# Attention in larger batches: regrouping the score and value steps of one layer, and sharing the softmax totals of four heads

## The chip, the cores and the metric

The kernel runs on one core of a Trainium2 chip. The metric is the device time of one execution in microseconds (us). The whole network is in float32, and every matrix product below is a float32 product.

The engines are named as the profile names them: PE is TensorE (its matrix products), PEld is TensorE loading the stationary operand, DVE is VectorE, ACT is ScalarE, POOL is GpSimd. PSUM is the memory that TensorE writes its products into; here it has eight banks, each 128 partitions by 512 float32 numbers.

## The reference, cut to what matters

The network has four layers for 8 samples of 512 channels by 32 x 32 positions. Only layer 0 is changed. Its attention has 8 heads of 64 channels over 1024 positions:

```python
h = group_norm(x, gn_scale, gn_bias)
qkv = jnp.einsum('oc,bchw->bohw', qkv_w, h) + qkv_b[None, :, None, None]
q, k, v = (to_heads(t) for t in jnp.split(qkv, 3, axis=1))      # 8 heads of 64
attn = jax.nn.softmax(jnp.einsum('bnsd,bntd->bnst', q, k) * hd ** -0.5, axis=-1)
h = jnp.einsum('bnst,bntd->bnsd', attn, v)
h_flat = h.transpose(0, 1, 3, 2).reshape(B, C, S).transpose(0, 2, 1)
for _ in range(3):                                               # lax.scan
    h_flat = h_flat + 0.1 * jnp.tanh(jnp.einsum('bsc,oc->bso', h_flat, inl_w) + inl_b)
h = h_flat.transpose(0, 2, 1).reshape(B, C, H, W)
x = x + jnp.einsum('oc,bchw->bohw', proj_w, h) + proj_b[None, :, None, None]
```

Layers 1 to 3 (another attention, an up- and downsampling filter, a convolution with mixed experts) follow and are as before.

## The kernel before

The exponentials are taken without subtracting a maximum. So the kernel looks at the sums it divides by: whatever is larger than a bound, or not a number, makes a second program run that subtracts the maximum. It collects what is to be looked at in `seen`. With these inputs the second program does not run.

For each sample, the attention of layer 0 is cut into 8 **groups**. A group is two heads (one on partitions 0 to 63, the other on 64 to 127) and one half (512) of the query positions. A group has 8 **steps**, one for each 128 key positions. A step computes the transposed scores (keys on partitions, queries along the free axis), their exponentials `e`, adds `e` to the group's running sum `acc` and multiplies `e` with the values. A "scores" product has 64 rows of the array for each head, so the two heads share the array by rows; an "av" product has 64 columns for each head, so they share it by columns.

```python
ps_sc = ...tile_pool(bufs=2, PSUM)   # 2 pairs of banks: [128, 1024]
ps_tp = ...tile_pool(bufs=2, PSUM)   # 2 single banks:   [128, 512]
ps_mm = ...tile_pool(bufs=2, PSUM)   # 2 single banks:   [128, 512]
def tmp(name, n=HALF):               # e: 5 buffers of [128, 1024]
    ...
def sums(name):                      # acc: 2 buffers of [128, 1024]
    return work.tile([P, S], F32, tag="sums", name=name, bufs=2)

# ---- in layer0 ----
groups = [(oc, sh) for sh in range(2) for oc in range(CC)]

def scores(t):
    g, jc = divmod(t, SC)                                   # SC = 8
    oc, sh = groups[g]
    ps = ps_sc.tile([P, S], F32, tag="scores", ...)         # a pair of banks
    scores_T([ps[:, ts(r, HALF)] for r in range(2)], ...)   # 64 x 128 by 64 x 512, both heads
    e = tmp(f"e_{b}_{t}", S)
    nc.scalar.activation(e, ps, AF.Exp, scale=HD ** -0.5)
    exps[t] = e
    if jc == 1:
        accs[g] = sums(f"acc_{b}_{g}")
        nc.vector.tensor_add(accs[g], exps[t - 1], e)
    elif jc > 1:
        nc.vector.tensor_add(accs[g], accs[g], e)

def weighted(t):
    ...
    for r in range(2):                                      # 128 x 64 by 128 x 512, both heads
        nc.tensor.matmul(avs[g][rows[r]], v[:, jc, ts(2 * oc + r, HD)], e[:, ts(r, HALF)],
                         start=(jc == 0), stop=(jc == SC - 1))

def normalised(g):
    oc, sh = groups[g]
    acc = accs.pop(g)
    ps = bank(ps_tp, f"total_{b}_{g}")
    for r in range(2):                                      # sums over the partitions
        nc.tensor.matmul(ps[rows[r]], ones[:, 0:HD], acc[:, ts(r, HALF)], start=True, stop=True)
    inv = tmp(f"inv_{b}_{g}", HALF)
    nc.vector.reciprocal(inv, ps)
    nc.vector.tensor_mul(hf[:, oc, ts(sh, HALF)], avs.pop(g), inv)
    for part in (acc[:, 0:HALF], acc[:, HALF:S], inv):
        nc.gpsimd.tensor_add(seen, seen, part)

n = len(groups) * SC
for t in range(0, n + 4, 2):            # two steps of scores, then the two steps of av before them
    for u in (t, t + 1):
        if u < n: scores(u)
    for u in (t - 2, t - 1):
        if 0 <= u < n: weighted(u)
    if t >= SC + 2 and (t - 2) % SC == 0:
        normalised((t - 2) // SC - 1)
```

After the attention come three "inl" products and "proj". Each multiplies 512 x 512 weights with the 512 x 1024 `hf` in seven products of quarters, not eight (Strassen's scheme in Winograd's form). The data side needs four sums of quarters, each in two parts, written by `quarter_sums`; for the first of the three, they are written over `v`:

```python
for cc in range(2):                      # in quarter_sums
    b11, b12 = src[:, cc, 0:HALF], src[:, cc, HALF:S]
    b21, b22 = src[:, cc + 2, 0:HALF], src[:, cc + 2, HALF:S]
    nc.vector.tensor_sub(t[0][cc], b12, b11)
    nc.vector.tensor_sub(t[1][cc], b22, t[0][cc])
    nc.vector.tensor_sub(t[2][cc], b22, b12)
    nc.vector.tensor_sub(t[3][cc], t[1][cc], b21)

order = (                                # in product: result, banks, weights, data (a number: that sum)
    ("P1", "A", "A11", b11), ("C11", "A", "A12", b21), ("U2", "X", "S2", 1),
    ("U3", "X", "S3", 2), ("C22", "Y", "S1", 0), ("C21", "X", "-A22", 3),
    ("C12", "Y", "S4", b22),
)
```

The framework in which the kernel is written places semaphores and buffers, and also chooses the order of instructions on each engine: it is near the order of the text, but an instruction whose buffer or input is not there yet by the framework's own estimate can be put behind a later one.

## Time and profile before

| | |
|---|---|
| time, median of 3 runs | 3939.58 us (3938.11 to 3940.49) |
| span of the profiled run | 3934.4 us |
| PE busy | 3868.2 us (98%) |
| DVE busy | 2593.8 us (66%) |
| ACT busy | 1105.0 us (28%) |
| POOL busy | 436.1 us (11%) |
| granted TensorE clock, mean | 0.998 |

The busy time of PE is a union: where two products share the array, their common time counts once. A busy PE is not an array that is full. The chain of waits follows the program back from its last instruction, at each step to what released it; the shares say on which engine's work the end rests. Rows of groups give the source line, the engine, the operation, the tiles written and read, the shapes, the count, the total busy time and the mean duration of one, and then the idle time of the engine just before them. In a timeline each row is a run of like instructions: start, length, engine, what it is, and in brackets the idle time before it and what ended that.

### The profile page before, as it was taken

The numbers are of one execution on the slowest core, as the hardware profiler recorded it, in microseconds if no ns is written. First come the engines' busy times: TensorE is split into PE (matmuls) and PEld (weight loads), VectorE is DVE, ScalarE is ACT, GpSimd is POOL, SyncE is SP. The second block draws the span as 40 slices with busy tenths as digits, with TensorE's granted clock in tenths as the row PEclk, the third lists the DMA queues.
The fourth block names the chain that finished last, engine by engine and source line by source line (L and its number), as shares of the span: only waits on it lengthen the run. The fifth ranks groups of instructions, "written<-read, shape, count | busy, mean of one in ns | idle before, by whom it ended". The sixth has DMA issues, their size and how long they took to land.

```text
span 3934.4 us, 37957 instructions
## 1 busy us (share of the span) xinstructions
PE 3868.2 (98%) x14630; PEld 2032.6 (52%) x14630; DVE 2593.8 (66%) x3690; ACT 1105.0 (28%) x1507; POOL 436.1 (11%) x310
## 2 busy tenths in 40 slices
PE   8999999999999999999999999999999999999998
PEld 4336653476435763366434754357534764346543
DVE  4777848764686647775586646765487655766786
ACT  1421224212332114212241123322142122421333
POOL 5310003000120003100030002200031001301000
PEclk9999999999999999999999999999999999999999
DMA  5002310122101310023101221013200131003432
GB/s 197 19 0 83 115 57 1 40 77 100 38 0 59 118 68 11 0 83 115 56 1 59 79 81 37 1 70 107 78 1 24 60 115 57 1 0 112 164 134 103
DMA packets 85792, 247.86 MB, mean 63 GB/s; under 512 B 10480, under 2 KB 33024, under 8 KB 78816
## 3 DMA queue, kind: packets, MB, share of 16 engines
q1 hardware_dynamic: 69712, 220.23, 15.8%
q10 hardware_dynamic: 13824, 12.59, 1.0%
q0 software_dynamic: 2064, 12.51, 0.8%
q8 instruction: 117, 1.92, 0.2%
q14 instruction: 75, 0.61, 0.0%
HBM read 185.40 MB, written 59.90 MB: 62 GB/s over the span
## 4 chain that ended last, share of the span: by engine, by line
PE 90%; DVE 7%; issue 1%; DMA 1%; ACT 1%; SPq 0%; DVEq 0%; ACTq 0%
PE scores L266 13%; PE av L627 11%; PE inl_X L414 6%; PE dn L941 6%; PE up L920 5%; PE v_X L414 4%; PE inl_Y L414 4%; PE av_X L854 4%; PE c L1150 3%; PE v_Y L414 3%; PE av_A L854 3%; PE v_A L414 3%; PE inl_A L414 3%; PE av_Y L854 2%; PE proj_X L414 2%; PE q_X L414 2%
## 5 line engine op out<-in xcount | busy, mean ns | idle before, releaser
L612 ACT ACTIVATE e<-scores 128x1024 f32<-128x1024 f32 x512 | 497.1, 1021 | 632.7 <-PE scores L266 632.0
L618 DVE TENSOR_TENSOR acc<-acc,e 128x1024 f32<-128x1024 f32 x384 | 494.1, 1287 | 122.7 <-ACT e L612 101.6
L266 PE MATMUL scores<-q,k 64*128 64x512 f32 x2048 | 511.0, 616 | 7.0 <-ACT e L612 3.6
L627 PE MATMUL av<-e,v 128*64 128x512 f32 x2048 | 494.1, 604 | 0.0
L644 POOL TENSOR_TENSOR seen<-seen,acc 128x512 f32<-128x512 f32 x128 | 212.3, 1659 | 1574.9 <-DVE acc L618 1569.9
L266 PEld LDWEIGHTS scores<-q,k 64*128 64x128 f32 x2048 | 175.7, 186 | 334.3 <-ACT e L612 163.2
L627 PEld LDWEIGHTS av<-e,v 128*64 128x64 f32 x2048 | 124.8, 136 | 338.8 <-issue 335.8
L941 PEld LDWEIGHTS dn<-dn_op,up 128*128 128x128 f32 (+1 forms) x2048 | 239.9, 192 | 46.3 <-issue 24.3
L904 DVE SCALAR_TENSOR_TENSOR up<-up,leak 128x512 f32<-128x512 f32 (+1 forms) x264 | 174.9, 687 | 132.9 <-ACT leak L903 124.9
L941 PE MATMUL dn<-dn_op,up 128*128 128x126 f32 (+5 forms) x2048 | 244.7, 275 | 10.1 <-DVE up L904 9.5
L903 ACT ACTIVATE leak<-up 128x512 f32<-128x512 f32 (+1 forms) x264 | 150.0, 595 | 248.9 <-DVE up L904 125.4
L641 DVE RECIPROCAL inv<-total 128x512 f32<-128x512 f32 x64 | 214.7, 3354 | 0.0
L920 PE MATMUL up<-halo,up_op 126*128 126x512 f32 (+1 forms) x384 | 182.8, 605 | 0.4 <-DVE up L904 0.3
L414 PE MATMUL inl_X<-T_hf,w_inl 128*128 128x512 f32 x384 | 172.6, 592 | 0.0
L644 POOL TENSOR_TENSOR seen<-seen,inv 128x512 f32<-128x512 f32 x64 | 125.1, 1955 | 417.6 <-DVE inv L641 417.6
L414 PE MATMUL inl_A<-hf,w_inl 128*128 128x512 f32 x384 | 169.5, 594 | 0.0
L616 DVE TENSOR_TENSOR acc<-e,e 128x1024 f32<-128x1024 f32 x64 | 85.0, 1329 | 102.4 <-ACT e L612 100.7
L508 ACT ACTIVATE inl_U<-inl_U,inl_b 128x512 f32<-128x512 f32 x96 | 64.0, 714 | 304.7 <-DVE inl_U L523 304.7
L519 DVE TENSOR_TENSOR inl_U<-inl_X,inl_P 128x512 f32<-128x512 f32 x96 | 61.8, 685 | 116.0 <-PE inl_X L414 116.0
L736 POOL TENSOR_TENSOR seen<-seen,acc 128x512 f32<-128x512 f32 x16 | 22.6, 1410 | 1019.9 <-DVE acc L728 1019.9
L1150 PE MATMUL c<-rim,mixed 128*128 128x512 f32 x288 | 124.9, 592 | 0.0
L414 PEld LDWEIGHTS inl_A<-hf,w_inl 128*128 128x128 f32 x384 | 72.3, 190 | 94.5 <-issue 88.8
(302 smaller groups left out, 5757.6 us busy)
## 6 DMA issues: line engine op xcount, KB each, us to landing
halo<-ypad_u SPq DMA_DIRECT2D x128, 252.0 KB
halo<-ypad_u SPq DMA_DIRECT2D x128, 198.0 KB
w_v<-stored_u_v SPq DMA_DIRECT2D x14, 1792.0 KB
x<-in_x_dram SPq DMA_DIRECT2D x32, 512.0 KB
spill_u<-z SPq DMA_DIRECT2D x28, 512.0 KB
z<-spill_u SPq DMA_DIRECT2D x28, 512.0 KB
out_dram<-z SPq DMA_DIRECT2D x28, 512.0 KB
w_q<-stored_u_q SPq DMA_DIRECT2D x7, 1792.0 KB
```

Of the source, the lines that this page charges most:

```text
L266: nc.tensor.matmul(ps[r], k[r], q[r], start=True, stop=(shift is None))
L414: nc.tensor.matmul(dst, lhs, rhs, start=(opens and s == 0 and cc == 0), stop=(cc == 1 and s == rows), skip_group_check=True,)
L612: nc.scalar.activation(e, ps, AF.Exp, scale=HD ** -0.5)
L618: nc.vector.tensor_add(accs[g], accs[g], e)
L627: nc.tensor.matmul(avs[g][rows[r]], v[:, jc, ts(2 * oc + r, HD)], e[:, ts(r, HALF)], start=(jc == 0), stop=(jc == SC - 1),)
L641: nc.vector.reciprocal(inv, ps)
L644: nc.gpsimd.tensor_add(seen, seen, part)
L854: nc.tensor.matmul(ps[:, ts(s, QR)], left[:, j, at : at + P], right[:, j, :], start=(what in ("P1", "U2", "W") and s == 0 and j == 0), sto ...
L904: nc.vector.scalar_tensor_tensor(dst, ps, SQRT2, t, ALU.mult, ALU.max)
L920: nc.tensor.matmul(ps[i], op[0 : IR * n, :], halo.tile(t)[0 : IR * n, c + i, :], start=True, stop=True,)
L941: nc.tensor.matmul(rows[:, r0 - first : r1 + 1 - first, c0 : c1 + 1], up[t][0:k, c, ts(cc, P)], op[:, r0 - 4 * t + 3 : r1 + 4 - 4 * t, c0 ...
L1150: nc.tensor.matmul(banks[g].rearrange("p (h w) -> p h w", w=W), wt[:, at : at + P], h1[:, ky + 16 * g : ky + 16 * g + 16, kx : kx + W], st ...
```

## The change

Six things change, all in layer 0 but for the last.

1. **Batches.** The 8 steps of a group are dealt with in batches of 3, 3 and 2: the scores of a batch, then the av products of the batch before. Three steps of scores need three pairs of banks where two are there, so steps 2 and 5 of each group take the two single banks of `ps_tp`, with two exponentials of 512 in place of one of 1024.
2. **Totals.** The totals of two groups (four heads) are computed together, in one bank, each on 32 columns of the array. One reciprocal, in place in PSUM, serves both groups.
3. **The av banks.** ScalarE copies a group's av result to `hf` as soon as it is there, unscaled, and so frees the bank. VectorE scales it in `hf` later. Since a head's total stands on 32 partitions and its result on 64, each head takes two multiplications on 32 partitions.
4. **The bounds check.** GpSimd no longer adds `acc` and the reciprocals to `seen`. The sum of `acc` along the free axis comes as an accumulator output of the last addition to it (now a scalar_tensor_tensor), and the sum of the reciprocals as that of a ScalarE copy of them; both go to columns of `seen_sums`, which are looked at with `seen`.
5. **The start of the first "inl" product.** C22, whose first sum needs no group after the sixth, is multiplied before U2 and U3. What is done with its result stays behind U3. The four sums are written in the order in which the products want them.
6. **Buffers.** `acc` has three buffers, not two.

The diff, without the comparison of `seen_sums` at its end and some blank lines (cuts are marked ...):

```diff
-        return work.tile([P, S], F32, tag="sums", name=name, bufs=2)
+        return work.tile([P, S], F32, tag="sums", name=name, bufs=3)
...
-        for cc in range(2):
+        turns = [(i, cc) for cc in range(2) for i in range(4)]
+        if into is not None:
+            turns.sort()
+        for i, cc in turns:
...
-            nc.vector.tensor_sub(t[0][cc], b12, b11)
-            nc.vector.tensor_sub(t[1][cc], b22, t[0][cc])
-            nc.vector.tensor_sub(t[2][cc], b22, b12)
-            nc.vector.tensor_sub(t[3][cc], t[1][cc], b21)
+            one, two = (
+                (b12, b11), (b22, t[0][cc]), (b22, b12), (t[1][cc], b21),
+            )[i]
+            nc.vector.tensor_sub(t[i][cc], one, two)
...
+        if t1_first:
+            order = order[:2] + order[4:5] + order[2:4] + order[5:]
...
             for u in range(2):
-                made(what, u, banks[key][u])
+                if not t1_first or what != "C22":
+                    made(what, u, banks[key][u])
+                if t1_first and what == "U3":
+                    made("C22", u, banks["Y"][u])
...
-            ps = ps_sc.tile([P, S], F32, tag="scores", name=f"scores_{b}_{t}")
+            split = jc in (2, 5)
+            if split:
+                ps = [bank(ps_tp, f"scores_{b}_{t}_{r}") for r in range(2)]
+            else:
+                pair = ps_sc.tile([P, S], F32, tag="scores", name=f"scores_{b}_{t}")
+                ps = [pair[:, ts(r, HALF)] for r in range(2)]
...
-            nc.scalar.activation(e, ps, AF.Exp, scale=HD ** -0.5)
+            if split:
+                for r in range(2):
+                    nc.scalar.activation(e[:, ts(r, HALF)], ps[r], AF.Exp, scale=HD ** -0.5)
+            else:
+                nc.scalar.activation(e, pair, AF.Exp, scale=HD ** -0.5)
...
-            elif jc > 1:
+            elif 1 < jc < SC - 1:
                 nc.vector.tensor_add(accs[g], accs[g], e)
+            elif jc == SC - 1:
+                nc.vector.scalar_tensor_tensor(
+                    accs[g], accs[g], 1.0, e, ALU.mult, ALU.add,
+                    accum_out=seen_sums[:, b, g : g + 1],
+                )
...
+        def apart(g):
+            oc, sh = groups[g]
+            nc.scalar.copy(hf[:, oc, ts(sh, HALF)], avs.pop(g))
+
         def normalised(g):
...
+            parts = [accs[i][:, ts(r, HALF)] for i in (g, g + 1) for r in range(2)]
             ps = bank(ps_tp, f"total_{b}_{g}")
-            for r in range(2):
-                nc.tensor.matmul(
-                    ps[rows[r]], ones[:, 0:HD], acc[:, ts(r, HALF)], start=True, stop=True
-                )
+            bands = [ps[32 * i : 32 * i + 32, :] for i in range(4)]
+            for band, part in zip(bands, parts):
+                nc.tensor.matmul(band, ones[:, 0:32], part, start=True, stop=True)
+            nc.vector.reciprocal(ps, ps)
+            for i, band in enumerate(bands):
+                oc, sh = groups[g + i // 2]
+                for at in (HD * (i % 2), HD * (i % 2) + 32):
+                    dst = hf[at : at + 32, oc, ts(sh, HALF)]
+                    nc.vector.tensor_mul(dst, band, dst)
             inv = tmp(f"inv_{b}_{g}", HALF)
-            nc.vector.reciprocal(inv, ps)
-            nc.vector.tensor_mul(hf[:, oc, ts(sh, HALF)], avs.pop(g), inv)
-            for part in (acc[:, 0:HALF], acc[:, HALF:S], inv):
-                nc.gpsimd.tensor_add(seen, seen, part)
-
-        n = len(groups) * SC
-        for t in range(0, n + 4, 2):
...
+            at = NG + g // 2
+            nc.scalar.activation(inv, ps, AF.Copy, accum_out=seen_sums[:, b, at : at + 1])
+
+        batches = [
+            range(g * SC + i, g * SC + j)
+            for g in range(len(groups)) for i, j in ((0, 3), (3, 6), (6, 8))
+        ]
+        for i in range(len(batches) + 1):
+            for t in batches[i] if i < len(batches) else ():
+                scores(t)
+            for t in batches[i - 1] if i else ():
+                weighted(t)
+            g, part = divmod(i, 3)
+            if g and part == 0:
+                apart(g - 1)
+            if g and g % 2 == 0 and (part == 1 or i == len(batches)):
+                normalised(g - 2)
...
-            all_of(product(name, w["inl"], hf, t, inner_step(name, hf), first_banks=banks))
+            all_of(product(name, w["inl"], hf, t, inner_step(name, hf), first_banks=banks,
+                           t1_first=(it == 0)))
```

## The prediction

> **What bounds the kernel now.** I read the page first, its busy times and the shares of the chain of waits:

> ```profile
> PE 3868.2 (98%) x14630; PEld 2032.6 (52%) x14630; DVE 2593.8 (66%) x3690; ACT 1105.0 (28%) x1507; POOL 436.1 (11%) x310
> ...
> PE 90%; DVE 7%; issue 1%; DMA 1%; ACT 1%; SPq 0%; DVEq 0%; ACTq 0%
> ```

> TensorE is the bound, so time can come only from fewer or fuller PE intervals, or from the few gaps between them. GpSimd at 11% is nowhere in the chain: the additions to `seen` that go away are worth nothing by themselves.

> Second, the chain in order of time, in the first sample's attention and in the product after it (start, length, what):

> ```profile
> 112.37 1.92 PE scores L266 x8
> 114.29 1.87 PE av L627 x8
> 117.01 1.92 PE scores L266 x8
> ...
> 133.01 1.92 PE scores L266 x8
> ...
> 249.11 6.87 PE inl_A L414 x16
> ```

> The last line gives the unit: 16 products that fill the array take 6.87 us, 0.429 each. Eight scores products on two halves of the array should take 4 x 0.429 = 1.72; they take 1.92. Eight av products should also take 1.72; they take 1.87. So each turn from av to scores costs 0.20 us and each turn from scores to av 0.15: **0.35 us an alternation**. From 114.29 + 1.87 = 116.16 to 117.01 PE does the totals of a group: **0.85 us**. From 117.01 to 133.01 is one group: 16.00 us = 4 x 3.79 + 0.85. No wait is in it; the attention of layer 0 runs as fast as PE does it in this order.

> Third, the timeline at one total and at the end of that attention (start, length, engine, what):

> ```profile
> 117.06 3.36 DVE L641 RECIPROCAL inv<-total 128x512 f32<-128x512 f32 x1
> ...
> 120.33 1.16 DVE L618 TENSOR_TENSOR acc<-acc,e 128x1024 f32<-128x1024 f32 x1
> ...
> 121.41 0.68 DVE L642 TENSOR_TENSOR hf<-av,inv 128x512 f32<-128x512 f32 x1
> ...
> 223.36 1.08 PE L637 MATMUL total<-acc,ones 128*64 128x512 f32 x4 [1.07 <-DVE acc L618]
> ...
> 224.37 7.13 PE L414 MATMUL inl_A<-hf,w_inl 128*128 128x512 f32 x16
> ...
> 231.34 1.02 PE L414 MATMUL inl_X<-v,w_inl 128*128 128x512 f32 x2
> ...
> 232.54 2.84 PE L414 MATMUL inl_X<-v,w_inl 128*128 128x512 f32 x6 [0.18 <-DVE v L379]
> ```

> Two things are to be seen. The addition at 120.33 stands before the multiplication though it is written after it, so the framework's reordering is at work. And at the end PE waits: 1.07 us for the last `acc`, then 232.54 - 231.34 - 2 x 0.429 = 0.34 us for the sums over `v`: **1.4 us a sample**.

> [...] The trace has 190 ns for 128 columns (inl_A) and 137 ns for 64 (total), a slope of 53 ns per 64[...]. So I estimate 137 - 27 = 110 ns for 32 columns, and four such loads at 0.44 us are just about one product's 0.429: four tiles should run nearly at full rate. [...]

> **The change, part by part.**
> - *Batches.* Three alternations a group, not four: 64 groups x 0.35 = **22 us** less, all on PE's path.
> - *Totals.* Two groups cost 2 x 0.85 = 1.70 now. After: 8 products on four tiles, 2 x 0.429 = 0.86, plus 0.15 for the turn from 64 to 32 columns, 1.01. 32 pairs x 0.69 = **22 us** less.
> - *End of the attention.* The last addition to `acc` no longer stands behind a reciprocal: total(4,5) is long past. PE does av products of five steps, about 4.4 us, between the last scores and the total; exponentials and additions of two steps need about 1.1 + 1.0 + 1.2 = 3.3. So the 1.07 should go. Then DVE needs 3.36 + 8 x 0.68 + 2 x 0.68 = 10.2 us from the total to the first sums that U2 needs, while PE has P1, C11 and now C22: 24 x 0.429 = 10.3. So the 0.34 should go too, just so. 8 x 1.4 = **11 us** less.
> - *VectorE.* In a pair of groups: 14 additions of 1.22 (undisturbed), one reciprocal 3.36, eight multiplications 5.4 (0.68 by the free size; a quarter of the partitions saves nothing), 25.9 us, with the two accumulator outputs about 26. The pair will last some 30.5. Before it was 2 x 12.75 of 2 x 16.00 (the window of the group at 117.01). Fuller, not the bound on average.
> - *ScalarE.* In a group: six exponentials at 0.97 (1.94 for two in the timeline), four halves at 0.6 (597 ns in layer 1), the copy 0.6 and half the summing copy: about 9.1 of 15.3. No bound.
> - *GpSimd.* 5.55 us of additions a group go (the same window). They slow VectorE where they overlap (three additions take 4.35, 1.45 each, beside 1.16 to 1.23 alone); that is slack, not path.

> Without a new wait: 22 + 22 + 11 = 55 us, **3884 us**.

> **The rivals.** *One: the bank of the total.* This is the one that I fear. A total takes one of the two `ps_tp` banks, and it is freed only after the reciprocal, all eight multiplications and ScalarE's copy. Step 2 of the next group takes both banks. Counted from the end of the total, PE has: scores of two steps 1.92, av of three 2.73, scores of the next group's first two 1.92: it arrives at step 2 after 6.6 us. VectorE has 3.36 + one addition that slips in, as at 120.33, 1.2 + 5.4 = 10.0 us. In the written order PE waits 3.4 us, three times a sample (the fourth total is the end): 24 x 3.4 = 82 us. That would eat everything: **3966 us**. Against it speaks that the framework reorders: the first head of step 2 goes alone into the free bank, the av products of the waiting batch go forward, the second head follows. A head alone fills half the array, 0.86 us more, and the split costs about one more alternation, 0.35: 1.2 x 24 = 29 us, **3913 us**. If it puts the whole step back cleanly, the loss is near zero.

> *Two: four tiles are no faster than two.* If loads or reads of four operands at once hold them to two at a time, a pair's totals take 1.71 + 0.15 and the 22 us become a loss of 5: **3911 us** without the first rival. For it: no trace of four tiles. Against it: the loads' estimate above, and two tiles running at exactly half the time.

> *Three: VectorE or the buffers of `e` become the bound.* Two batches of three hold six `e`, with five buffers. The third exponential of steps 3 to 5 then waits for the first av product after the scores, some 1 us. PE is by then in 2.7 us of av products and needs that `e` only a batch later: hidden. VectorE falls behind by 10 us at a total and has until the next, 30 us later, with 15% slack: hidden unless the accumulator outputs cost far more than the addition.

> **Range and chances.** I give the clean case (3884) about 35%, the split step (3913) 45%, the written order with its wait (3966, or part of it) 20%. Weighted, that is 3913. The gains may be some us larger than counted, as small waits at the start and in U3 are left out; I take 9 us off and say **3904 us**, 0.9% less than before. Low end 3872: the clean case with a dozen us more. High end 3950: waits at about half the steps of the first rival, or both first rivals in part. Over 2% faster means under 3861, 79 us, more than all the counted gains: 4%. Over 2% slower means over 4018, which needs waits that I don't find: 1%. Within 2%: 95%.

> **What would show it.** In the chain: scores in runs of 12 and 8 products at about 2.8 and 1.9 us, av likewise. Totals: eight 128x32 products in about 0.9 us; 1.7 would show the second rival. PE's idle before scores of step 2, or runs of scores of two products alone after each total, would show the first, with VectorE's `hf` multiplications as the releaser. DVE: `hf<-total,hf` 32x512, 256 of them at about 0.68. POOL's rows of L644 gone. A group from total to total: about 30.5 us for two. At the end of the attention no idle before the total and before inl_X. The prediction is wrong above all if the multiplications take much more or less than 0.68 us, or if the framework's order leaves PE idle.

## The result: slower by 2.7%, and the profile after

The changed kernel takes **4048.16 us** (median of 4 runs, 4042.92 to 4053.32), against 3940.03 us: the ratio is 1.0275, with a 95% interval of 1.0257 to 1.0293. The prediction said 3904 us, in a range of 3872 to 3950.

First the page of the changed kernel: the busy times, the shares of the chain of waits, and three rows of groups (line, engine, operation, tiles, shapes, count | busy us, mean ns | idle us before, and what ended it).

```profile
PE 3911.7 (97%) x14630; PEld 2053.9 (51%) x14630; DVE 2579.2 (64%) x3918; ACT 1172.5 (29%) x1763; POOL 99.2 (2%) x118
...
PE 88%; DVE 8%; issue 3%; ACT 1%; DMA 1%; SPq 0%; ACTq 0%; DVEq 0%
...
L270 PE MATMUL scores<-q,k 64*128 64x512 f32 x2048 | 528.3, 617 | 61.1 <-ACT inv L679 57.6
...
L675 DVE TENSOR_TENSOR hf<-total,hf 32x512 f32<-32x512 f32 x256 | 175.5, 685 | 3.5
...
L670 DVE RECIPROCAL total<-total 128x512 f32<-128x512 f32 x32 | 107.7, 3367 | 30.2 <-PE total L669 30.2
```

GpSimd's additions are gone (POOL 436.1 to 99.2 us), the multiplications cost what was expected (685 ns each on 32 partitions; the 128x512 ones of the kernel before have a median of 678), and PE is no less busy: it has 43.5 us **more** busy time, though the change takes work and turns away from it. And the scores wait 57.6 us for `inv`, ScalarE's copy of the reciprocals, which is the last reader of the total's bank. The view of PE's waits has that first (waiter, releaser, us in all, times, longest) and a second one that is new:

```profile
PE scores L270 <- ACT inv L679: 57.6, 24, 2.4
PE inl_X L424 <- DVE T_hf L388: 12.4, 8, 1.6
```

24 is three a sample: the fourth total of a sample is followed by no scores. Here is one of the 24 in PE's timeline of the first sample (start, length, what, in brackets the idle time before):

```profile
133.76 1.06 PE L669 MATMUL total<-acc,ones 128*32 128x512 f32 x8
134.76 1.99 PE L270 MATMUL scores<-q,k 64*128 64x512 f32 x8
136.68 2.79 PE L654 MATMUL av<-e,v 128*64 128x512 f32 x12
139.40 2.84 PE L270 MATMUL scores<-q,k 64*128 64x512 f32 x10
142.17 1.07 PE L654 MATMUL av<-e,v 128*64 128x512 f32 x2
145.65 1.12 PE L270 MATMUL scores<-q,k 64*128 64x512 f32 x2 [2.40 <-ACT inv L679]
146.70 1.93 PE L654 MATMUL av<-e,v 128*64 128x512 f32 x6
148.56 2.85 PE L270 MATMUL scores<-q,k 64*128 64x512 f32 x12
```

A float32 product appears as two instructions (the 8 x 8 x 8 steps of two heads are 1024 scores products, x2048 in the row above; what the prediction calls a product, 0.429 us with the array full, is one of these), so x4 is one step, both heads. The fourth line has x10: two whole steps, and **one head alone** of step 2, which goes into the free bank of `ps_tp`. Then one head alone of an av step (x2 in 1.07), then 2.40 us of nothing, then the other head of step 2, and the other av head. A head alone takes as long as two together: the ten at 139.40 last 2.84 us, the twelve at 148.56 2.85. And this is what holds the bank meanwhile, in the timelines of DVE and ScalarE:

```profile
134.90 3.37 DVE L670 RECIPROCAL total<-total 128x512 f32<-128x512 f32 x1 [0.39 <-PE total L669]
...
138.17 1.21 DVE L640 TENSOR_TENSOR acc<-acc,e 128x1024 f32<-128x1024 f32 x1
139.29 5.58 DVE L675 TENSOR_TENSOR hf<-total,hf 32x512 f32<-32x512 f32 x8
...
144.91 0.60 ACT L679 ACTIVATE inv<-total 128x512 f32<-128x512 f32 x1 [2.39 <-DVE hf L675]
145.40 0.19 ACT L679 ACTIVATION_READ_ACCUMULATOR inv<-total 128x1 f32 x1
```

From 134.90 to 144.87 VectorE, then 0.7 us ScalarE: the bank is held 10.7 us.

I measured each stage in every sample from the starts of PE's products. Summed over the 8 samples, before and after:

| stage | before, us | after, us | difference |
|---|---|---|---|
| layer 0's attention, first scores to last av | 1021.4 | 1108.1 | +86.7 |
| from there to the first inl product | 21.4 | 12.1 | -9.3 |
| the three inl products | 577.8 | 597.8 | +20.0 |
| last proj product to layer 1's last scores | 290.2 | 286.7 | -3.5 |
| from there to layer 2's last dn product | 980.3 | 994.8 | +14.5 |

The other stages add 4.3 us; the spans differ by 112.7. So there are three things to explain: attention, which should have fallen by 44, the inl products, and the last row, with layer 1's av products and layer 2 (products "up", then "dn"), in which nothing of the computation has changed. I call this row layer 2 below.

### The profile page after: what moved, and what is told of

It reads as the page before. It is cut to its first block, busy times and chain, and to the rows that moved or that the text cites. A ratio compares the mean times of both kernels' runs of the same rounds, so it can differ in the third digit from the quotient of the medians.

```text
span 4047.1 us, 37953 instructions
## 1 busy us (share of the span) xinstructions
PE 3911.7 (97%) x14630; PEld 2053.9 (51%) x14630; DVE 2579.2 (64%) x3918; ACT 1172.5 (29%) x1763; POOL 99.2 (2%) x118
## 3 DMA queue, kind: packets, MB, share of 16 engines
q1 hardware_dynamic: 69712, 220.23, 15.3%
q8 instruction: 117, 1.92, 0.2%
## 4 chain that ended last, share of the span: by engine, by line
PE 88%; DVE 8%; issue 3%; ACT 1%; DMA 1%; SPq 0%; ACTq 0%; DVEq 0%
PE scores L270 11%; PE av L654 10%; PE inl_X L424 6%; PE dn L983 6%; PE up L962 5%; PE v_X L424 4%; PE inl_Y L424 4%; PE av_X L896 4%; PE inl_A L424 3%; PE c L1197 3%; DVE hf L675 3%; PE v_Y L424 3%; PE av_A L896 3%; PE av_Y L896 2%; PE v_A L424 2%
## 5 line engine op out<-in xcount | busy, mean ns | idle before, releaser
L270 PE MATMUL scores<-q,k 64*128 64x512 f32 x2048 | 528.3, 617 | 61.1 <-ACT inv L679 57.6
L654 PE MATMUL av<-e,v 128*64 128x512 f32 x2048 | 526.3, 618 | 0.0
L640 DVE TENSOR_TENSOR acc<-acc,e 128x1024 f32<-128x1024 f32 x320 | 392.5, 1227 | 194.0 <-ACT e L634 161.0
L634 ACT ACTIVATE e<-scores 128x1024 f32<-128x1024 f32 x384 | 373.3, 1023 | 454.0 <-PE scores L270 453.9
L270 PEld LDWEIGHTS scores<-q,k 64*128 64x128 f32 x2048 | 194.1, 189 | 396.3 <-issue 243.9
L424 PE MATMUL inl_X<-T_hf,w_inl 128*128 128x512 f32 x384 | 177.6, 598 | 12.4 <-DVE T_hf L388 12.4
L675 DVE TENSOR_TENSOR hf<-total,hf 32x512 f32<-32x512 f32 x256 | 175.5, 685 | 3.5
L632 ACT ACTIVATE e<-scores 128x512 f32<-128x512 f32 x256 | 141.7, 599 | 69.6 <-PE av L654 46.7
L670 DVE RECIPROCAL total<-total 128x512 f32<-128x512 f32 x32 | 107.7, 3367 | 30.2 <-PE total L669 30.2
L424 PEld LDWEIGHTS inl_X<-T_hf,w_inl 128*128 128x128 f32 x384 | 70.5, 189 | 110.4 <-issue 65.1
L896 PE MATMUL av_X<-v,eT 128*128 128x256 f32 x512 | 122.5, 386 | 2.1 <-DVE av_W L875 1.2
L424 PEld LDWEIGHTS inl_A<-hf,w_inl 128*128 128x128 f32 x384 | 72.3, 190 | 94.8 <-issue 81.6
```

Of the source, the lines that this page charges most:

```text
L270: nc.tensor.matmul(ps[r], k[r], q[r], start=True, stop=(shift is None))
L424: nc.tensor.matmul(dst, lhs, rhs, start=(opens and s == 0 and cc == 0), stop=(cc == 1 and s == rows), skip_group_check=True,)
L634: nc.scalar.activation(e, pair, AF.Exp, scale=HD ** -0.5)
L675: nc.vector.tensor_mul(dst, band, dst)
L896: nc.tensor.matmul(ps[:, ts(s, QR)], left[:, j, at : at + P], right[:, j, :], start=(what in ("P1", "U2", "W") and s == 0 and j == 0), sto ...
```

## Experiments

| kernel | edit | time, us | ratio to before, 95% |
|---|---|---|---|
| e1_av_bank | changed kernel, totals in another pool of banks | 3928.8 | 0.9969 to 0.9986 |
| e2_old_order | changed kernel without part 5 | 4077.6 | 1.0331 to 1.0365 |
| e3_both | both edits | 3948.0 | 1.0018 to 1.0035 |
| e4_no_copy | changed kernel without ScalarE's copy of the reciprocals | 4067.6 | 1.0314 to 1.0349 |
| e5_batches | kernel before, with part 1 alone | 3911.8 | 0.9914 to 0.9951 |
| e6_pairs | e1 in batches of two steps | 3949.6 | 1.0013 to 1.0031 |
| e7_copy_first | e1, ScalarE's copy ahead of the multiplications | 3920.6 | 0.9930 to 0.9969 |
| e9_last_apart_old_order | e7 without part 5, last two groups' totals singly | 3930.2 | 0.9968 to 0.9985 |
| e10_three_sums | kernel before, with part 6 alone | 3951.5 | 1.0019 to 1.0042 |
| e11_best | e9, its two copies late, layer 2's buffers as before | 3915.6 | 0.9916 to 0.9962 |
| e12_new_order | kernel before, with part 5 alone | 3955.0 | 1.0025 to 1.0050 |
| e13_filler | changed kernel, with 24 x 3 repeated score steps | 4015.5 | 1.0168 to 1.0202 |

My theories have letters in the expectations. A: the total's bank is what costs the time. B: VectorE falls behind, whichever bank the total stands in. C: it is the new order of the inl products that makes them longer. D: they are longer because VectorE now has 9 us of work after the attention's end. E: layer 2 moved through the third buffer of part 6. F: part of the loss is TensorE's clock.

### The bank of the total

`ps_mm` also has two banks, for the av results, and part 3 frees each of them early. So the total can stand there:

```diff
-            ps = bank(ps_tp, f"total_{b}_{g}")
+            ps = bank(name=f"total_{b}_{g}")      # ps_mm
```

> The changed kernel with the four-head total in one of the two banks of the av products, not in one of the two banks that steps 2 and 5 of a group use. Theory A (the bank): TensorE waits because the total's bank is held for 10 us by the reciprocal, an addition, eight multiplications and the copy. Then all 24 waits of 2.4 us before scores go, the scores and av products stand together again, and the stretches of half TensorE clock that follow the waits go (102 us of them now, 21 before): the attention of a sample falls from about 139 to 121 us, and the kernel from 4048 to about 3905 us. Theory B (VectorE falls behind): the burst of 10 us on VectorE delays the additions, and with them the buffers of e and acc, whichever bank the total stands in: then the waits stay, under other names, and the time stays above 4020 us.

**3928.8 us: 119 us less from one argument.** Attention is 990.2 us for 8 samples instead of 1108.1, and the wait is gone from the view of waits; VectorE has the same work to do, so theory B falls. The order of the text is kept (PE's timeline of this kernel, at the place of the changed kernel's 139.40):

```profile
138.23 2.85 PE L270 MATMUL scores<-q,k 64*128 64x512 f32 x12
141.00 1.94 PE L654 MATMUL av<-e,v 128*64 128x512 f32 x8
142.87 3.69 PE L270 MATMUL scores<-q,k 64*128 64x512 f32 x12
```

Three steps in 2.85 us, as they should be. The third line, three steps in 3.69, has one head alone again: 0.85 us that come back three times a sample. What holds the array there is e7's subject.

### Is it the wait alone? The copy, the filler and the clock

Without ScalarE's copy the bank comes free earlier:

```diff
-            inv = tmp(f"inv_{b}_{g}", HALF)
-            at = NG + g // 2
-            nc.scalar.activation(inv, ps, AF.Copy, accum_out=seen_sums[:, b, at : at + 1])
```

(This leaves the sum of the reciprocals out of the bounds check.)

> The changed kernel without ScalarE's summing copy of the reciprocals (the check of the reciprocals is left out). Theory A: the bank is now freed by the last multiplication, about 10.1 us after the total's end, not 0.7 us later; the scores that wait follow their first head at once, with about 2.5 us of idle before them, and VectorE's multiplication as the releaser; the av product that stood alone in each wait rejoins its other head. About 1.1 us less at each of 24 waits and some half-clock stretches fewer: 4010 to 4025 us. Theory B: no change from 4048 us, as VectorE has as much to do.

The expectation missed: 4067.6 us, **19 us slower than with the copy**. The bank is held 0.7 us less, but PE does no av half first, and the wait is 2.68 us. A pair of groups, from total to total, takes 34.37 us in e4 where the clock holds, 0.72 less than the 35.09 of the changed kernel, so the earlier bank is worth 24 x 0.72 = 17 us. More than that is lost again. What differs is the granted clock, 0.978 in the mean against 0.988 of the changed kernel and 0.998 before. In the trace's record of the granted clock, e4 has 180.7 us at half clock, the changed kernel 102.2, the kernel before 21.3. In attention the stretches are 3.4 or 6.8 us long: 23 of e4's 24 waits are followed by such a stretch (143.4 us), 13 of the changed kernel's 24 (64.9 us), and none before. The changed kernel's second wait ends at 180.73. First the row of PE's timeline after it, then the windows (window, its length, busy us of PE, PEld, DVE, ACT, POOL with counts, PEclk, the DMAs' share and rate):

```profile
181.79 3.45 PE L654 MATMUL av<-e,v 128*64 128x512 f32 x6
```

```profile
175.60:181.70 6.10, 3.70 (x12) 0.91 (x8) 5.99 (x10) 3.11 (x5) 0.00 (x0) 1.00 0.00 0
181.79:185.16 3.37, 3.37 (x7) 0.65 (x6) 1.80 (x2) 0.60 (x1) 0.00 (x0) 0.54 0.00 0
185.16:188.50 3.34, 3.34 (x15) 1.39 (x16) 0.91 (x1) 2.52 (x3) 0.00 (x0) 0.95 0.02 5
```

The same six instructions took 1.93 us at 146.70, after the first wait. In the first of the three windows PE is busy for 3.70 of 6.10 us, most of them with half of the array; in the second the clock is 0.54 and PE is "busy" all the time. Halves and half clock count as busy time: no view of waits can show them.

The stretches lie on a grid: all 37 starts and ends of stretches in the changed kernel's trace (without the trace's own end) are within 0.001 us of one grid of 3.4133 us. And 2.40 us of idle time, with half-filled products on both sides, were followed by half clock in 13 of 24 cases.

Which 13 is told by where a wait falls on that grid. A line of the grid cuts the wait that ends at 145.65 into 1.26 and 1.14 us, and no half clock follows; of the wait that ends at 180.73, 2.09 us fall into one interval, and the next interval runs at half clock. In the changed kernel half clock followed where at least 1.50 us of the wait fell into one interval (13 waits) and never where it was at most 1.42 (11). In e2 below, with the same 24 waits, it was 1.46 or more (17) and at most 1.44 (7). (In e4 the two overlap a little: 1.43 to 2.68 in the 23, 1.49 in the one without.) So how many waits are hit depends on their position too, not on their length alone. The spread of the four runs goes with the clock: 4042.9 us at a mean of 0.989, 4053.3 at 0.986. Nothing here separates the idle time from the half-filled products beside it.

To separate the clock from the wait, I gave PE **more** work: a score step ahead of each wait is repeated three times, with the same operands into the same bank.

```diff
+            for _ in range(3 if g in (3, 5, 7) and jc == 1 else 0):
+                scores_T(ps, ...)                   # as just before, again
             e = tmp(f"e_{b}_{t}", S)
```

> The changed kernel with three repeats of one pair of score products (the step just ahead of each wait for the total's bank, 24 in all, 3 x 0.86 us each, same operands and same bank, so nothing else is computed). They go where TensorE stands idle for 2.40 us or works with one head alone, and the total still frees its bank at the same moment. What it tells apart: theory F, that a part of the changed kernel's loss is the clock, granted at half after each of these waits (102 us at half clock, 21 before): the idle time falls to about 0.9 us per wait, half clock falls to 20 to 40 us, and the kernel with MORE work is faster than the changed one, 4000 to 4015 us. The rival, that waits alone cost the time and half clock is only where the waits are: the repeats fill idle time and change nothing, 4045 to 4050, or make it slower where they run past the wait.

**4015.5 us, 33 us faster for 72 more score steps.** PE's timeline of this kernel at the second total:

```profile
172.98 5.41 PE L270 MATMUL scores<-q,k 64*128 64x512 f32 x22
179.23 1.12 PE L270 MATMUL scores<-q,k 64*128 64x512 f32 x2 [0.83 <-ACT inv L688]
180.28 1.94 PE L663 MATMUL av<-e,v 128*64 128x512 f32 x8
```

The idle time is 0.83 us, no half clock is left in attention (39.8 us in the whole program), and both full pairs of groups in every sample, from total to total, take 35.09 us. In the changed kernel the pairs take 35.08 or 35.09 where the clock holds, and 36.7 to 38.4 where it doesn't. So 35.09 holds the wait and the halves, and the clock comes on top: attention 1108.1 - 1078.3 = **29.8 us**, near half of the 64.9 us at half clock. The rival, that waits alone cost the time, expected 4045 us or more.

### What is left in e1: a copy in front of the exponentials

In e1 the copy of the reciprocals still follows all the multiplications. It waits for them on ScalarE, and the exponentials behind it wait too, so that the scores' banks come free late. It needs only the reciprocals:

```diff
             nc.vector.reciprocal(ps, ps)
+            inv = tmp(f"inv_{b}_{g}", HALF)
+            nc.scalar.activation(inv, ps, AF.Copy, accum_out=...)
             for i, band in enumerate(bands):
                 ...                                 # the eight multiplications
-            inv = ...
-            nc.scalar.activation(inv, ps, AF.Copy, accum_out=...)
```

> The total in a bank of the av products, and ScalarE's summing copy ahead of the eight multiplications, not behind them. Theory A': what is left in the attention after the bank was moved (three stretches a sample of 12 scores products in 3.64 us, not 2.78) is ScalarE standing behind that copy, which waits for the last multiplication. Then these go: 3 x 0.86 x 8 = 20 us less than 3929, 3909 us, the attention of a sample 121.1 us for 123.7. If the split steps are late because VectorE is behind, nothing changes, or it gets worse, as the multiplications now wait for the copy.

3920.6 us. Attention is 969.8 us, 121.1 in most samples, and a pair of groups takes 30.57 us, not 31.42: the 0.85 us is gone. The row at the place of e1's 142.87 is whole again:

```profile
142.93 2.85 PE L270 MATMUL scores<-q,k 64*128 64x512 f32 x12
```

This is the attention that the prediction meant, with "about 30.5 us for two". The total time is less good than expected, since the inl products have grown to 75.9 us a sample.

### Batches alone, totals alone

Part 1 in the kernel before, with each group's total by itself, after the second batch of the next group:

```diff
+            split = jc in (2, 5)
...
+        batches = [... ((0, 3), (3, 6), (6, 8))]
...
+            if g and (part == 1 or i == len(batches)):
+                normalised(g - 1)
```

> The kernel before with the batches of 3, 3 and 2 alone: steps 2 and 5 in the two single banks, the totals of each group as before (two heads, reciprocal to SBUF, one multiplication), after the second batch of the next group. The price of an alternation, 0.35 us: one fewer in each of 64 groups is 22 us, so 3916 us, the attention of a sample at about 124.7 us for 127.5. The total holds its bank only for the reciprocal, 3.4 us, and step 2 comes 6.6 us later: no wait. If on the other hand the batches themselves cost (two exponentials of 512 for one of 1024, six e in five buffers), the gain is smaller or gone: 3930 us or more.

**3911.8 us, the lowest median of all kernels** (e11's 3915.6 is not clearly apart from it). Attention falls by 27.4 us in 8 samples. In its steady part two groups take 31.29 us instead of 32.00: 0.355 a group for the 0.35 of an alternation, 22.7 us in all; the rest falls at the start and the end of a sample's attention. Its PE timeline has the run lengths expected, and a single group's total:

```profile
113.82 2.85 PE L266 MATMUL scores<-q,k 64*128 64x512 f32 x12
116.59 2.79 PE L636 MATMUL av<-e,v 128*64 128x512 f32 x12
119.22 1.03 PE L646 MATMUL total<-acc,ones 128*64 128x512 f32 x4
```

The other half, the shared totals with batches of two steps (no step needs `ps_tp` any more; parts 3 to 6 are still in):

```diff
-            split = jc in (2, 5)
+            split = False
...
-            for g in range(len(groups)) for i, j in ((0, 3), (3, 6), (6, 8))
+            range(g * SC + i, g * SC + i + 2) for g in range(len(groups)) for i in (0, 2, 4, 6)
```

> The changed kernel, its total in a bank of the av products, but in pairs of steps as before, all scores in pairs of banks: four-head totals, copies and accumulator outputs without the batches. If the price of an alternation is right, the attention is 8 x 0.35 = 2.8 us a sample longer for it, and 2.6 us shorter because no split step finds its bank late: within 5 us of the run with the total in an av bank, 3929 us. If the batches give nothing, it is 20 us faster than that run.

3949.6 us: attention falls by 11.9 us only, as the scores wait 12.9 us in all for exponentials (3.6 in the kernel before). That this is ScalarE's late copy again is likely after e7, but no run shows it here. The totals don't pay for what comes with them elsewhere, which is next.

### The inl products: a repair of something new

Part 5 undone in the changed kernel, and in e1 (the edit is the same two hunks):

```diff
-        if into is not None:
-            turns.sort()
...
-            all_of(product(name, w["inl"], hf, t, inner_step(name, hf), first_banks=banks,
-                           t1_first=(it == 0)))
+            all_of(product(name, w["inl"], hf, t, inner_step(name, hf), first_banks=banks))
```

> The changed kernel with the first inl product and its sums in the order of before (C22 after U3, the sums by halves); all else as changed. Theory C: the new order is what makes the three inl products 2.5 us a sample longer (72.2 to 74.7), since P1 of the second inl product is pulled ahead and TensorE then waits 1.56 us for the sums of the second. Then that wait goes: 20 us less, minus up to 10 us if the wait before the first U2 comes back: 4028 to 4040 us. If the longer inl stage has another cause (the accumulator outputs, the copies), it stays and the time is 4048 us.

> Both of these at once: the total in a bank of the av products, the first inl product in the old order. Theories A and C together: about 3890 us, 1.3% less than before the change. Theory B: above 4000 us.

Theory C falls: without part 5 both kernels are slower, 4077.6 against 4048.2 and 3948.0 against 3928.8. The inl products take 77.6 us a sample, not 74.7. (Of e2's 29 us, 13 lie in attention, where 95.6 us ran at half clock and not 64.9; e3 has none of that.) PE's timeline of e2 shows what the new order covers:

```profile
245.05 1.10 PE L422 MATMUL inl_X<-v,w_inl 128*128 128x512 f32 x2 [2.88 <-DVE v L386]
```

After the last total VectorE has a reciprocal of 3.37 and eight multiplications of 5.6 before it can write the sums; the kernel before has 3.36 + 0.68 there. So part 5 repairs a wait that part 2 makes. What it costs by itself is shown by putting it, alone, into the kernel before:

> The kernel before with part 5 alone: T1 and C22 of the first inl layer moved forward, and the sums by quarter. Theory D: the new order takes a product of the second inl layer between U2 and U3 of the first, so that it trades the wait at the end of attention (1.2 us per sample) for a wait of 1.6 us at the second layer's sums and for turns between forms: inl 74.7 us instead of 72.2, tail shorter by about 1, so 3950 us (+8 to +15). The prediction's own account, that the new order only covers waits: tail 1.5 instead of 2.7 us, inl as before, 3930.

3955.0 us: inl 74.7 us a sample instead of 72.2, with the wait before the total as before. The timeline of e12 has the reason:

```profile
248.41 3.60 PE L419 MATMUL inl_Y<-hf,w_inl 128*128 128x512 f32 x8
251.85 3.60 PE L419 MATMUL inl_A<-hf,w_inl 128*128 128x512 f32 x8
257.00 1.12 PE L419 MATMUL inl_X<-T_hf,w_inl 128*128 128x512 f32 x2 [1.56 <-DVE T_hf L384]
```

In the kernel before 16 `inl_A` products stand ahead of this `inl_X` (the prediction's line at 249.11), and they cover the second layer's sums. Here only 8 do: the framework has put the other 8 into the first layer, 4 before and 4 after U3, where their bank was free. PE waits 1.56 us, 12.5 in all; and the changed kernel has the same wait, the 12.4 us of the view above.

Theory D, the old order with the last two groups' totals taken singly (one reciprocal and one multiplication of 128 partitions each, so that VectorE has 4 us after the attention as before):

```diff
+            if g == last and part == 1:
+                normalised_one(g - 1)
+            if i == len(batches):
+                normalised_one(last)
```

> As the run before, and in addition the totals of the last two groups one by one, each on 64 columns with one reciprocal and one multiplication of 128 partitions, so that only 4 us of VectorE work lie between the attention's end and the sums, not 9; the first inl product in the old order. Theory D: both orders of the first inl product pay for the late eight multiplications, the old one with 2.9 us of waiting at its U2, the new one because P1 of the second product goes ahead and leaves too little to cover the second product's sums (1.56 us of waiting, 1 us of turns). Then the three inl products are back at 72.2 us a sample (74.7, or 77.6 in the old order): 20 us less, plus 0.7 us a sample for the two extra totals: about 3895 us. If the longer inl stage has to do with the order alone, the old order gives 77.6 again and about 3935 us.

Inl is back at 72.0 us: D holds for the old order, which pays only where VectorE is late (77.6 in e2, 72.2 before). The new order costs 74.7 with the late multiplications and without them (e12), so there D is not the cause. The time, 3930.2, is 10 us above e7's, as the single total's copy on ScalarE stood in front of the last exponentials, and the last av products waited for them, 2.70 us a sample.

### Layer 2, and all together

One number in the kernel before:

```diff
-        return work.tile([P, S], F32, tag="sums", name=name, bufs=2)
+        return work.tile([P, S], F32, tag="sums", name=name, bufs=3)
```

> The kernel before with one edit: three buffers under the name sums instead of two. Nothing else is changed, and nothing needs the third buffer. In all variants built on the changed kernel, but not in the one that only put batches into the kernel before, layer 2's up part was 49.6 instead of 51.2 us and its dn part 72.2 to 73.9 instead of 68.5 us. Theory E: it is the third buffer: the statistics of the next sample, which take a buffer of that name, are placed one product group earlier, so that the first up products come two av products sooner and wait for the halo's transfer. Theory E expects dn at 72 to 74 us, up at 49.6, nothing in layer 0, and 3955 us (+12 to +20). The rival, that the summing in the attention moved layer 2 in another way: 3940, dn at 68.5.

3951.5 us, **12 us slower for a buffer that nobody needs**; all stages up to layer 1's last scores are the same to 0.1 us. From there to the first `up` product most samples take 49.6 us instead of 51.2, but from that to the last `dn` product 72.3 instead of 67.8 to 70.1 (the expectations call these two "up" and "dn"). The next sample's statistics also use a buffer of that name. PE's timeline around the first `up` product of a sample, first in the kernel before, then in e10:

```profile
1782.88 3.62 PE L854 MATMUL av_X<-v,eT 128*128 128x256 f32 x16
1786.33 0.28 PE L288 MATMUL gn_mean<-mv,group_mean 128*128 128x4 f32 x2
1786.47 1.10 PE L920 MATMUL up<-halo,up_left_op 99*128 99x512 f32 x2
```

```profile
1786.38 1.03 PE L854 MATMUL av_X<-v,eT 128*128 128x256 f32 x4
1787.24 0.28 PE L288 MATMUL gn_mean<-mv,group_mean 128*128 128x4 f32 x2
1789.08 1.10 PE L920 MATMUL up<-halo,up_left_op 99*128 99x512 f32 x2 [1.56 <-DMA halo<-ypad_u]
```

The framework places `gn_mean` and the `up` product 12 instructions (x4 instead of x16) earlier among layer 1's av products, and PE stands in front of a transfer that isn't there yet. Such waits are 9.7 us in e10 and 2.5 before, of the 11.8 that the row grows by. Theory E holds. The way from the third buffer to that place, through the framework's own estimate, stays open.

Last, all of it: e9 with both copies of the single totals after the last of them, and every third `acc` under a name of its own:

```diff
-                accs[g] = sums(f"acc_{b}_{g}")            # 3 buffers
+                accs[g] = (acc_tile if g % 3 == 2 else sums)(f"acc_{b}_{g}")   # 1 and 2 buffers
```

> The changed kernel with all that the runs so far point to: the totals in the bank of the ordinary products, ScalarE's summing copy ahead of the eight multiplications, the last two groups' totals singly with both copies after the last one, the inl layers in their old order, and the third accumulator under a name of its own so that layer 2 keeps two buffers under the name sums. Theory A with C, D and E: attention 122 us per sample (121.1 with the pairs alone), the three inl layers 72.2, up 51.2, dn 68.5, so 6 us per sample less than before: 3895 us (3885 to 3905). If the last single totals stall the attention as in the run before: attention 125, 3920. If layer 2 still shifts: 3912.

3915.6 us, not 3895. Layer 2 is as before (E again), inl at 72 to 74, attention 976.7; but the step from the attention to inl is 4.7 to 5.6 us instead of 2.7. VectorE's timeline shows it:

```profile
213.80 3.37 DVE L694 RECIPROCAL total<-total 128x512 f32<-128x512 f32 x1
217.08 1.21 DVE L641 TENSOR_TENSOR acc<-acc,e 128x1024 f32<-128x1024 f32 x1
218.20 0.68 DVE L696 TENSOR_TENSOR hf<-total,hf 128x512 f32<-128x512 f32 x1
218.79 1.22 DVE L643 SCALAR_TENSOR_TENSOR acc<-acc,e 128x1024 f32<-128x1024 f32 x1
```

The reciprocal of the group before the last stands in front of the last additions, and the last total waits 3.1 us for them (24.5 in all). It is the same kind of wait that the change was to remove. So in this kernel the shared totals give 17 us in attention over e5 (976.7 against 994.0) and lose 19 after it (39.4 us from the attention to inl against 20.8): nothing is left of them beside the batches. Whether an order without this last wait would keep the 17 us, no run shows.

## Why the prediction was wrong, point by point

- **Batches, 22 us: right.** 22.7 us in the steady part of e5, 27.4 in all. What makes a turn cost this, no run shows.
- **Totals on four tiles: right in itself.** From the start of the eight products to the scores behind them it was 0.99 or 1.00 us in the changed kernel, for 1.01 predicted; a weight load of 32 columns 108 ns for an estimated 110 (from those of 128 and 64 columns, 190 and 137 ns). The second rival did not occur. With the bank elsewhere and the copy early (e7), a pair of groups went from 32.00 to 30.57 us: 32 x 1.43 = 46 us for the 44 of the two steps (51.6 with the start and the end of the attention).
- **The multiplications: right.** 0.685 us each. They start 0.70 us apart, each 14 ns after the end of the last (5.58 us for eight). Other multiplications, additions and subtractions of 512 columns on all 128 partitions, equally long, start 0.60 apart when one follows another at once (`inl_U<-inl_X,inl_P`, one operand in PSUM, 0.61), before the end of the last. So each multiplication costs some 0.1 us more than one of those, an estimate from these starts (what keeps them apart was not shown): small, but not nothing.
- **Rival One: right mechanism, and in it the step that failed.** VectorE held the bank 9.97 us of the 10.0 predicted. ScalarE's copy, the last reader, was named but left out of the sum (0.7 us). The step that failed reads: "Against it speaks that the framework reorders", which put the split step at 1.2 x 24 = 29 us, with 45%, and took the av products of the waiting batch to cover the wait. It did split the step, just as described, but only **one av half** went forward, for the other head's scores stood ahead of the rest. So PE reached the second head 8.4 us after the total, when the bank had 2.4 us to go. A pair of groups costs 35.09 - 30.57 = 4.52 us more: 2.40 idle, 2 x 0.86 for the halves and about 0.35 for a turn make 4.47. Times 24 that is 108 us, above even the 82 of the written order (98 with the copy in it): a partial reordering cost the wait **and** the halves.
- **The clock: missing.** 29.8 us in attention. Nothing in the prediction lets a wait cost more than its length.
- **ScalarE "no bound": true of the average only.** In e1 the copy that waits in its queue holds back the exponentials, 0.85 x 24 = 20 us, and e7 takes them back. In the changed kernel the row at 148.56 is whole (2.85 us), so there it adds nothing of its own.
- **End of the attention, 11 us: right there, and paid back behind it.** PE has no idle time before the total or U2; 9.3 us less between attention and inl. But C22 ahead of U2 let the framework move half of the second layer's `inl_A` products forward: inl is 20.0 us longer, of which 12.4 are the new wait (3.5 come back in the row of layer 1's scores, in e12 too; alone, part 5 costs 15.5 us). "Just so" looked at the first wait behind the moved work and not at the next.
- **Buffers: no step at all.** The third buffer got no line in the sum. It costs 12 us in layer 2 by itself; the changed kernel's is 14.5 us longer.
- **Third rival: not met.** No wait for `e` buffers or VectorE's load inside the attention shows in the changed kernel.

Together: 3884 + 108 (bank) + 30 (clock) + 20 (inl) + 14.5 (layer 2) is about 4056; attention without the waits was 8 us better than the sum and layer 1's scores are 3.5 us shorter, which leaves 4045 of the measured 4048. The range was too narrow since it took the first rival as the one thing that could go wrong, and counted it as idle time only.

## What to carry to other kernels

When several results share one bank, add up everything that must happen before its **last** reader is through, on every engine, and compare it with when the next writer arrives. If the first is later, take another bank rather than hope for a reordering. Count a wait of TensorE with what stands around it: here half-filled products and half clock made 2.40 us of waiting cost 4.52 and, on average, 1.2 more. And a change of order or of a buffer's count needs a look at the next stages too, for their order may change with it.
